# Gate and up products of two experts in one product of 512 moving columns

## The chip, the cores and the metric

The kernel runs on one NeuronCore of a Trainium2 chip. The metric is the time of one execution on the device in microseconds (us), lower being better. The kernel before takes 586.83 us, the median of three runs (585.6 to 587.18). Engines are named as in the profile: PE (TensorE: matrix products, PEld being its weight loads), DVE (VectorE), ACT (ScalarE), POOL (GpSimd) and SP (SyncE, which issues the DMAs).

## The reference

One layer of a perceiver: 256 tokens `x` of width 512 and a context of 25088 rows of width 512. Three blocks, each with a layer norm ahead of it and added to `x`: attention with a sigmoid over the context, causal self-attention with 16 heads, and a feed-forward block of 8 experts. The change touches the last:

```python
logits = jnp.einsum('th,eh->te', xf, gate_w)
onehot = one_hot(argmax(logits, -1), 8)
g = jnp.einsum('th,ehd->etd', xf, wg)        # gate, 8 experts of [512, 128]
u = jnp.einsum('th,ehd->etd', xf, wu)        # up
inter = jnp.square(jax.nn.relu(g)) * u
inter = inter * onehot.T[:, :, None]
out = jnp.einsum('etd,edh->th', inter, wd)   # down, [128, 512] each
```

All eight experts are computed for all tokens; the one-hot factor leaves one of them per token.

## The kernel before

**Split products.** Most large products are made in an fp32r form in which an operand is split into a high part and a low part (`split`, lines 62 to 65: ACT makes the high part, L64, DVE the rest, L65). A product is then three matmuls (`mm3`, lines L68 to L70): high by high, high by low, low by high. Each matmul has a weight load of its own, of 128x128.

**The main loop** goes over the context in 49 chunks of 512 rows. A chunk is loaded twice, transposed and plain (1 MB each), split, projected to keys, scored against the queries, and its sigmoid weights multiply the plain rows into two accumulators `acc`, one per tile of 128 tokens. From the third chunk on, `prepare` does one piece of side work a chunk: it loads 512 columns of a weight matrix that is needed later, splits it, and writes the two halves to a DRAM tensor (`spill`), in pieces of 256 KB on SP's queue. The list `todo` says at which column each half goes: `to` for the high half and `to + apart` for the low half.

**The tail** works on two tiles of 128 tokens, `tt` = 0 and 1. Its order on every engine is the order of the calls at the end of the body, held by `in_order`. The split expert weights come back from DRAM in eight loads of 1 MB (`load_gu`), into one tile `gu[e]` for each `e`. Before, the 2048 columns of `gu[e]` are the high half and the low half of expert `e`; in each half, four blocks of 256 columns follow each other, one for each 128 rows of the contraction, and a block holds 128 gate columns and 128 up columns.

**The experts** go in pairs (0 and 1, 2 and 3, ...). For each pair and token tile:
- `GU(tt, e, 0)` and `GU(tt, e, 1)`: the gate and up products. The normed tokens (`yhl`, high and low) are the weights of the array, the expert weights move through it. Both calls write one PSUM bank of 512 columns, 256 for each expert. For the last pair of the second tile the calls carry `alone`, and each has a bank of its own.
- `GE`: ACT takes the relu, DVE multiplies relu, gate, up and the one-hot factor.
- `IT`: PE transposes the result, ACT and DVE split it into `ft`.
- `DN`: the down product, 6 matmuls of 512 columns for a pair, added up over the experts in `fo`.

The calls are interleaved, so that other PE work stands between a pair's steps; the first gate/up calls lie between transposes and value products of the second tile's attention. The activation of `GE` reads both halves of the bank:

```python
nc.scalar.activation(r[:, ks], p4[:, ks, 0, :], AF.Relu)
```

`ks` covers both experts, except in the last pair. The order of the tail around a pair:

```python
GU(1, 2, 1)
DN(1, 0)
GE(1, 2)
GU(1, 4, 0)
IT(1, 2)
```

Of the kernel before, what the change touches and what calls it, by code (L numbers as in the profile page):

```python
# [22 lines left out]
D = 512  # L23
KD = D // P
# [4 lines left out]
E = 8  # L29
# [19 lines left out]
def body(ctx, tc, a, out, nch=NCH):  # L49
# [17 lines left out]
    def mm3(ps, ahi, alo, bhi, blo, first, last):  # L67
        mm(ps, lhsT=ahi, rhs=bhi, start=first, stop=False)  # L68
        mm(ps, lhsT=ahi, rhs=blo, start=False, stop=False)  # L69
        mm(ps, lhsT=alo, rhs=bhi, start=False, stop=last)  # L70

    def pair(name, shape, tag=None, bufs=1):
        return [sb.tile(shape, F32R, tag=f"{tag or name}{i}", name=f"{name}_{i}", bufs=bufs) for i in range(2)]

    def bank(name):
        return psum.tile([P, D], F32, tag="b", name=name, bufs=6)
# [4 lines left out]
    def toks(t):  # L81
        return slice(t * P, (t + 1) * P)
# [22 lines left out]
    spill = {n: dram.tile([P, 2 * w], F32, name=f"sp_{n}") for n, w in (("wo", KD * D), ("gu", E * 2 * D), ("dn", E * D))}  # L105

    todo = [("wv", at, None, at) for at in range(0, KD * D, D)]
    todo += [("gu", at, 2 * D, at // (2 * D) * 4 * D + at % (2 * D)) for at in range(0, E * 2 * D, D)]
    todo += [("dn", at, D, 2 * at) for at in range(0, E * D, D)]
    todo += [("wo", at, KD * D, at) for at in range(0, KD * D, D)]  # L110

# [194 lines left out]
    for i in range(2):  # L306
        nc.gpsimd.memset(kbd[i], 0.0)
    sums = sm.tile([P, 2, NH], F32, name="sums")


    gu, dn = [None] * E, [None] * E
# [203 lines left out]
    gps, inter = {}, {}  # L515

    def GU(tt, e, i, alone=False):
        if i == 0 or alone:
            gps[tt, e, i] = bank(f"gu{tt}_{e}_{i}").rearrange("p (e w) -> p e w", e=2)
        gps[tt, e, 1] = gps[tt, e, i]  # L520
        w = gu[e + i]
        for j in range(KD):
            s = slice(2 * j * P, 2 * (j + 1) * P)
            mm3(gps[tt, e, i][:, i, :], yhl[0][:, j, toks(tt)], yhl[1][:, j, toks(tt)], w[:, 0, s], w[:, 1, s],
                j == 0, j == KD - 1)

    def GE(tt, e, ks=slice(0, 2)):
# [96 lines left out]
    yhl = pair("y", [P, KD, T], "oh")  # L624
# [25 lines left out]
    PT(1, 5)  # L650
    PT(1, 6)
    GU(0, 0, 0)
    PV(1, 5)
    PT(1, 7)
    R1(1)
    GU(0, 0, 1)
    PV(1, 6)
    PV(1, 7)
    R2(1)
    GU(0, 2, 0)  # L660
    AT(1)
    LG(0)
# [108 lines left out]
```

## Time and profile before

| | |
|---|---|
| median of three runs | 586.83 us (585.6, 586.83, 587.18) |
| profiled execution | 586.28 us, its span 584.5 us |
| PE / PEld / DVE / ACT / POOL busy | 570.6 / 481.7 / 459.7 / 395.1 / 21.1 us |
| gate/up matmuls, 256 columns | 192, from 537.4 to 577.5 us |
| down matmuls, 512 columns | 48, from 552.3 to 580.4 us |
| loads of the split gate/up weights | 8, issued 464.9 to 493.4 us, 4.7 to 7.9 us to landing |
| spill writes of gate/up halves | 32, issued 80.6 to 226.7 us, 2.1 to 7.9 us to landing |

The span runs from the first to the last instruction of the core, and times in the profile count from its start. "L68" is a line of the kernel; `mm3` records all its matmuls under its own three lines, so groups are told apart by the tiles that they write (`gu`, `fo`, `acc`). [...] The lines of the profile stand in the prediction.

### The profile page before, as it was taken

Reading aid. Unit: us, or ns where it says so; the run is one execution under the profiler, and the core shown is the slowest. Engines: PE = TensorE matmul, PEld = TensorE weight load, DVE = VectorE, ACT = ScalarE, POOL = GpSimd, SP = SyncE. Lnnn points to the kernel's source line nnn. Section 1 sums busy time; section 2 is a strip of 40 time slices with the busy share of each in tenths; the row PEclk is TensorE's granted clock in tenths of the full one; section 3 lists DMA queues with packets and bytes.
Section 4 is the critical chain, followed back from the end, with each engine's and each line's share of the span. In section 5 each row is a group of like instructions: output and inputs, shape, how many; then the busy total and the mean of one; then the engine's idle time right before and its main releaser. Section 6 shows DMA issues by size and latency. Waiting matters only on the chain.

```text
span 584.5 us, 8061 instructions
## 1 busy us (share of the span) xinstructions
PE 570.6 (98%) x3036; PEld 481.7 (82%) x3036; DVE 459.7 (79%) x528; ACT 395.1 (68%) x512; POOL 21.1 (4%) x28
## 2 busy tenths in 40 slices
PE   4999999999999999999999999999999999999997
PEld 3888888888888888888888888888888887876996
DVE  6898888888888888888888888787878765667543
ACT  5877777777777777777777776767676752574211
POOL 5200000000000000000000000000000041000000
PEclk9999999999999999999999999999999999999999
DMA  8897887879888888788988887565657477700000
GB/s 288 334 368 283 278 295 281 321 278 317 287 324 276 325 271 325 266 337 298 332 282 319 274 337 245 208 225 206 234 198 243 149 295 262 316 1 1 1 1 36
DMA packets 33526, 144.94 MB, mean 248 GB/s; under 512 B 4240, under 2 KB 4432, under 8 KB 19792
## 3 DMA queue, kind: packets, MB, share of 16 engines
q1 hardware_dynamic: 33488, 144.44, 69.3%
q8 instruction: 23, 0.38, 0.2%
q14 instruction: 15, 0.12, 0.1%
HBM read 129.22 MB, written 15.20 MB: 247 GB/s over the span
## 4 chain that ended last, share of the span: by engine, by line
PE 95%; DVE 3%; DMA 1%; issue 0%; POOL 0%; ACT 0%; SPq 0%; POOLq 0%
PE acc L68 15%; PE acc L69 15%; PE acc L70 15%; PE kp_ps L70 8%; PE kp_ps L69 8%; PE kp_ps L68 8%; PE sc L70 4%; PE sc L69 4%; PE sc L68 4%; PE s L428 2%; PE gu L68 1%; PE gu L69 1%; PE gu L70 1%; PE pt L445 1%; DMA wq_r<-in_wq 1%; PE pv L456 1%
## 5 line engine op out<-in xcount | busy, mean ns | idle before, releaser
L68 PE MATMUL acc<-N,z 128*128 128x512 f32 x392 | 153.9, 393 | 0.0
L69 PE MATMUL acc<-N,z 128*128 128x512 f32 x392 | 153.7, 392 | 0.0
L65 DVE TENSOR_TENSOR N<-rN,N 128x2048 fp32r<-128x2048 f32 (+1 forms) x53 | 111.6, 2110 | 52.3 <-ACT N L64 52.2
L70 PE MATMUL acc<-N,z 128*128 128x512 f32 x392 | 152.5, 389 | 0.0
L65 DVE TENSOR_TENSOR T<-rT,T 128x2048 fp32r<-128x2048 f32 (+1 forms) x49 | 110.3, 2252 | 15.3 <-ACT T L64 15.3
L187 ACT ACTIVATE z<-sc 128x512 f32<-128x512 f32 x98 | 58.7, 599 | 66.5 <-PE sc L70 66.2
L64 ACT CAST N<-rN 128x2048 fp32r<-128x2048 f32 (+1 forms) x55 | 94.4, 1725 | 6.1
L64 ACT CAST T<-rT 128x2048 fp32r<-128x2048 f32 (+1 forms) x55 | 94.3, 1721 | 0.9 <-DMA rT<-in_ctxT 0.7
L70 PEld LDWEIGHTS acc<-N,z 128*128 128x128 f32 x392 | 73.6, 188 | 16.0
L68 PEld LDWEIGHTS acc<-N,z 128*128 128x128 f32 x392 | 74.0, 189 | 12.3
L69 PEld LDWEIGHTS acc<-N,z 128*128 128x128 f32 x392 | 74.0, 189 | 11.7
L68 PE MATMUL kp_ps<-T,wk 128*128 128x512 f32 x196 | 76.9, 392 | 0.0
L70 PE MATMUL kp_ps<-T,wk 128*128 128x512 f32 x196 | 76.7, 392 | 0.0
L69 PE MATMUL kp_ps<-T,wk 128*128 128x512 f32 x192 | 74.7, 389 | 0.0
L189 DVE TENSOR_TENSOR zacc<-zacc,z 128x512 f32<-128x512 f32 x98 | 67.2, 686 | 3.7 <-ACT z L187 1.7
L65 DVE TENSOR_TENSOR z<-z,z 128x512 fp32r<-128x512 f32 x98 | 67.3, 686 | 0.0
L64 ACT CAST z<-z 128x512 fp32r<-128x512 f32 x98 | 61.0, 623 | 3.1
L178 ACT ACTIVATE kp<-kp_ps,bk 128x512 fp32r<-128x512 f32 x49 | 33.9, 691 | 39.9 <-PE kp_ps L70 39.9
L70 PE MATMUL sc<-qp,kp 128*128 128x256 f32 x196 | 55.8, 285 | 0.1
L69 PE MATMUL sc<-qp,kp 128*128 128x256 f32 x196 | 55.4, 283 | 0.0
L68 PE MATMUL sc<-qp,kp 128*128 128x256 f32 x196 | 54.9, 280 | 0.0
L68 PEld LDWEIGHTS kp_ps<-T,wk 128*128 128x128 f32 x196 | 37.1, 189 | 7.8
(177 smaller groups left out, 658.5 us busy)
## 6 DMA issues: line engine op xcount, KB each, us to landing
rN<-in_ctxN SPq DMA_DIRECT2D x49, 1024.0 KB, 5.7
rT<-in_ctxT SPq DMA_DIRECT2D x47, 1024.0 KB, 5.5
sp_gu<-w_gu SPq DMA_DIRECT2D x32, 256.0 KB, 4.3
gu<-sp_gu SPq DMA_DIRECT2D x8, 1024.0 KB, 6.0
r_gu<-in_gu SPq DMA_DIRECT2D x16, 256.0 KB, 5.7
sp_dn<-w_dn SPq DMA_DIRECT2D x16, 256.0 KB, 4.3
dn<-sp_dn SPq DMA_DIRECT2D x16, 256.0 KB, 6.0
r_dn<-in_dn SPq DMA_DIRECT2D x8, 256.0 KB, 6.1
```

The lines of the kernel that those rows point to most:

```text
L64: copy(hi, src)
L65: eng.tensor_tensor(lo, src, f(hi), ALU.subtract)
L68: mm(ps, lhsT=ahi, rhs=bhi, start=first, stop=False)
L69: mm(ps, lhsT=ahi, rhs=blo, start=False, stop=False)
L70: mm(ps, lhsT=alo, rhs=bhi, start=False, stop=last)
L178: nc.scalar.activation(kp[c][0], ps, AF.Identity, bias=bk)
L187: nc.scalar.activation(z, ps, AF.Sigmoid, scale=1.0 / math.sqrt(128.0))
L189: tt2(zacc, zacc, z, ALU.add)
L428: mm(p3[:, h - h0:h - h0 + 2, :], lhsT=qs[:, tt, h // 2, g, :], rhs=kbd[g // 2][:, g % 2, h:h + 2, :nk], start=tt == 1, stop=tt == 0 and h ...
L445: nc.tensor.transpose(ps[:, toks(i * (tt + 1) + kt)], pr[tt, u][:, i, toks(kt)], ident)
L456: mm(pv[tt][r, g, :], lhsT=vs[kt][:, g * P + r.start:g * P + r.stop], rhs=pt[tt, u][:, toks(i * (tt + 1) + kt)], start=kt == 0, stop=kt == tt)
```

## The change

The DRAM layout of the split gate/up weights is regrouped by pairs: for a pair `e`, `e + 1`, the tile `gu[e]` now holds the high halves of both experts, and `gu[e + 1]` the low halves of both. Sizes, loads and their order stay.

A call of `GU` that is not `alone` now takes both experts at once: the moving operand is `gu[e][:, 0:2, s]`, two runs of 256 columns that lie 1024 columns apart, and the output is the whole bank of 512 columns. The first call of a pair does the contraction blocks 0 and 1, the second the blocks 2 and 3. Each such call has 6 matmuls of 512 columns in place of 12 of 256. The two calls with `alone` keep 12 matmuls of 256 columns, taken from the new places.

```diff
-    todo += [("gu", at, 2 * D, at // (2 * D) * 4 * D + at % (2 * D)) for at in range(0, E * 2 * D, D)]
+    todo += [("gu", at, 4 * D, at // (4 * D) * 8 * D + at % (4 * D)) for at in range(0, E * 2 * D, D)]
...
         gps[tt, e, 1] = gps[tt, e, i]
-        w = gu[e + i]
-        for j in range(KD):
+
+        for j in (range(KD) if alone else (2 * i, 2 * i + 1)):
             s = slice(2 * j * P, 2 * (j + 1) * P)
-            mm3(gps[tt, e, i][:, i, :], yhl[0][:, j, toks(tt)], yhl[1][:, j, toks(tt)], w[:, 0, s], w[:, 1, s],
+            k = slice(i, i + 1) if alone else slice(0, 2)
+            mm3(gps[tt, e, i][:, k, :], yhl[0][:, j, toks(tt)], yhl[1][:, j, toks(tt)], gu[e][:, k, s], gu[e + 1][:, k, s],
                 j == 0, j == KD - 1)
```

## The prediction

> **What bounds the kernel now.** I read the page first: the busy line, the clock row and the chain that ended last. Lines left out are marked.
>
> ```profile
> PE 570.6 (98%) x3036; PEld 481.7 (82%) x3036; DVE 459.7 (79%) x528; ACT 395.1 (68%) x512; POOL 21.1 (4%) x28
> ...
> PEclk9999999999999999999999999999999999999999
> ...
> PE 95%; DVE 3%; DMA 1%; issue 0%; POOL 0%; ACT 0%; SPq 0%; POOLq 0%
> ```
>
> TensorE (PE) is busy for 98% of the span, its clock is full in every slice, and the chain is 95% PE. An average can hide a stage with another limit, so I cut the span at the stage that the change touches. In the table of stretches the columns are length, then busy time (and count) of PE, PEld, DVE, ACT and POOL, then clock, DMA share and GB/s.
>
> ```profile
> 460.00:537.00 77.00, 75.30 (x473) 58.39 (x472) 51.72 (x93) 41.92 (x109) 9.51 (x8) 1.00 0.47 177
> 537.00:578.00 41.00, 41.00 (x315) 38.05 (x314) 20.17 (x56) 9.10 (x25) 0.55 (x1) 1.00 0.02 7
> 578.00:584.50 6.50, 2.83 (x14) 1.90 (x12) 1.92 (x5) 0.68 (x3) 0.00 (x0) 1.00 0.10 40
> ```
>
> The changed products all lie in the second row. There PE has no gap at all (41.00 of 41.00 us), DVE and ACT are half idle or more, and the DMA engines are nearly silent. So what PE saves there comes off the end, unless a wait appears where none is now.
>
> What is a matmul worth? The group rows give about 283 to 298 ns for a gate/up matmul of 256 columns and about 392 to 405 ns for one of 512. Those are latencies that overlap, and taken as costs they would promise 84 x (2 x 288 - 397) = 15 us. The true price is the distance between starts, so I read PE's timeline and the stretches of whole calls. First a down call (6 matmuls of 512 columns), then the gate/up call behind it (12 of 256), then the transpose that follows:
>
> ```profile
> 568.71:570.09 1.38, 1.38 (x8) 1.13 (x7) 0.73 (x3) 0.38 (x1) 0.00 (x0) 1.00 0.00 0
> 570.09:571.53 1.44, 1.44 (x13) 1.43 (x12) 0.30 (x2) 0.00 (x0) 0.00 (x0) 1.00 0.00 0
> ```
>
> ```profile
> 570.09 0.28 PE L68 MATMUL gu<-gu,y 128*128 128x256 f32 x1
> 570.21 0.28 PE L69 MATMUL gu<-gu,y 128*128 128x256 f32 x1
> ...
> 571.53 0.38 PE L541 MATMUL it<-ident,f 128*128 128x128 f32 x2
> ```
>
> Each matmul lasts 0.28 us, but the next starts 0.12 us later. The undisturbed gate/up calls take 1.44, 1.44 and 1.43 us (starts 562.56, 570.09, 574.58): 1.437/12 = 119.7 ns per matmul. The down calls at 561.17, 565.66, 568.71 and 573.19 take 1.39, 1.39, 1.38 and 1.39 us: 1.3875/6 = 231.3 ns. Both shapes move the same columns in a call: 12 x 256 = 6 x 512. The weight loads fill all of the 256-column call (1.43 us) and 1.13 of 1.38 us of the 512-column one; in both they lie under matmuls.
>
> **What the Trainium skill says.** "TensorE: Matmul & The Clock Gate", section "Back-to-back issue gap", prices an isolated warm gap at N/2.4 + 2.5 ns: about 109 ns for 256 columns and 216 for 512. So one 512 saves only one fixed issue cost (2.5 ns) against two 256. The trace agrees in kind and is dearer: 119.7 and 231.3, a saving of 2 x 119.7 - 231.3 = 8.1 ns. The measured pair is used. The same page, section "Step-by-step: what each phase is for", says that weight loads are pulled ahead of running matmuls; the trace shows this too. "SBUF — State Buffer" says that strided reads pay when successive accesses leave a 16-byte line, and that non-contiguous PSUM patterns slow matmuls. Here each run of the moving operand is 256 fp32 (1 KB), with one jump between two runs, and the output is a whole contiguous bank, so neither should bite. No row of before shows a split-weight product with this exact operand.
>
> **The change part by part.**
> 1. The calls. Of the 16 calls of the gate/up function, 14 change from 12 matmuls of 256 columns to 6 of 512: 168 matmuls and their weight loads become 84. The last two, marked alone, keep 12 of 256 (24 matmuls). Removed: 168 x 119.7 ns = 20.11 us. Added: 84 x 231.3 ns = 19.43 us. Sum: -0.68 us, or 49 ns a call. The first matmul behind a short PE operation has a bubble (0.20 instead of 0.12 us to the next after the transpose at 564.00; 0.31 instead of 0.23 us in the down call at 579.20): 0.08 us for either width, with as many such places as before, so nothing.
> 2. The moving operand in two runs, 4 KB apart in the partition. Its cost is unknown for these products. The nearest rows are attention scores for the first token tile (two runs of 128 columns, plain fp32) against the second (one run of 512):
>
> ```profile
> 505.14 1.03 PE L428 MATMUL s<-kbd,qs 128*128 128x256 f32 x4
> 506.00 0.38 PE L426 MATMUL s<-mask,identb 128*128 128x512 bf16 x1
> ...
> 521.17 1.02 PE L428 MATMUL s<-kbd,qs 128*128 128x512 f32 x2
> 522.03 0.27 PE L431 MATMUL s<-mask,identb 128*128 128x256 bf16 x1
> ```
>
> Four passes of 256 take 0.86 us, two of 512 take 0.86 us: a jump costs nothing visible. These passes run at about half the rate, which could hide a jump; the bf16 mask product (the same 128 columns four times, so four runs) starts at 504.93 and gives way at 505.14: 512 columns in 0.21 us. I take 0. Bounds: -15.6 ns per matmul (231.3 becomes the page's 215.7), which adds 1.3 us of gain as an estimate from that page; above, 8.1 ns, where two runs cost as much as two matmuls and the gain is gone. More than that no row suggests.
> 3. Order of accumulation. The first call of a pair now takes half the contraction for both experts, and the second call the rest. The activation behind a pair waits for both calls before and after, so it is not later. The first call needs two weight tiles instead of one; the eight loads are issued between 464.9 and 493.4 us and land within 7.9 us, the first use is at 537.4: 36 us of cover.
> 4. Addresses of the spilled halves in DRAM. 32 writes of 256 KB and 8 loads of 1 MB stay, with the same run lengths, order and queue; nothing passes anything else on SP's queue. They issue at 80.6 to 226.7 us and land in 7.9 us at most. A staging buffer is taken again two chunks later, and a chunk lasts about 9.8 us ((460-20)/45), so a slow write must lose some 10 us to be seen. Cost 0.
> 5. Cover that shrinks. A call is 49 ns shorter, so what hides under it has 49 ns less. No new wait is added, but on PE's in-order queue a late input would hold all that follows. The tightest place is the down product at 565.66, whose transposed input DVE finishes at 564.87 + 0.42 = 565.29: 0.37 us of slack becomes 0.32. At 568.71 and 573.19 it is 0.42. The transposes of the second tile's attention at 542.22 need a copy that DVE ends at 541.62: 0.60 becomes 0.50 behind two shorter calls. All hold, so cost 0; if one failed it would give back at most a call's 0.05 us.
>
> Sum: -0.68 us. Against the profiled execution: span 584.5 to 583.8, its time 586.28 (1.78 us around the span, which nothing touches) to 585.6. The shown runs are 585.6, 586.83 and 587.18; the profiled execution is 0.55 below their median. From the median: 586.83 - 0.7 = 586.1.
>
> **The rivals.**
> A. Larger gain. 512-column products run at 215.7 ns. Gain 84 x (239.4 - 215.7) = 2.0 us, 584.8. Against: the 48 down matmuls, with the same fp32r type and alternating weights, keep 231 ns, as do the main loop's products.
> B. Gain swallowed. A chain of transpose, ACT, DVE and down product becomes the bound, and PE waits for the 49 ns of each call: 586.8. For it: these chains are the only waits near. Against: the smallest slack that is left, 0.32 us, is over six times the step.
> C. Slower. The jump stalls the moving stream in all 84 products. Place: PE between 537 and 572 us. It is slower than before from 8.1 ns each, and by over 0.3% (1.76 us) from (1.76 + 0.68)/84 = 29 ns: 260 ns per matmul, 588.6. Against: the rows of point 2.
> That the change doesn't do what it says is excluded for counts and widths, which the code fixes; only its worth is open.
>
> **How the numbers follow.** About 0.3% is what a measurement of this kernel can tell from no change. Chances: the small gain 0.74, B 0.12, A 0.06, C 0.05, and 0.03 that medians of few runs (they spread over 1.6 us before) make the small gain look over 0.3%. The first two fall within 0.3%: 0.86; A and the spread make faster 0.09; C is slower 0.05. The small gain with the spread of the runs gives 585.3 to 586.9; the range reaches 585.0 towards A and 587.3 for B with a high run.
>
> **What would show it.** Right: 84 gate/up matmuls of 512 columns 230 to 233 ns apart, calls of 1.39 us, the stage 0.7 us shorter, PE still without gaps. Wrong: starts over 240 ns apart (C), 216 to 220 (A), PE idle before a down product or a transpose (B), or a main loop that moves by more than 0.3 us (point 4).

## The result and the profile after

The changed kernel takes 585.03 us (median of 22 runs, 584.1 to 585.89), the kernel before 586.05 us (also the median of 22 runs). The ratio is 0.9982, with a 95% interval of 0.9975 to 0.9988: faster by 0.12 to 0.25%. The profiled execution has a span of 582.7 us, against 584.5.

The page of the changed kernel, its busy line, clock and chain:

```profile
PE 568.9 (98%) x2952; PEld 476.3 (82%) x2952; DVE 459.9 (79%) x528; ACT 395.1 (68%) x512; POOL 21.2 (4%) x28
...
PEclk9999999999999999999999999999999999999999
...
PE 94%; DVE 3%; DMA 1%; issue 0%; POOL 0%; ACT 0%; SPq 0%; POOLq 0%
```

84 matmuls and 84 weight loads are gone (3036 to 2952), and PE still carries the chain. For the stage itself, the fairest stretch runs from the start of the first gate/up matmul to the start of the last down matmul. In the table of stretches of the kernel before:

```profile
537.43:580.43 43.00, 43.00 (x322) 39.52 (x321) 20.97 (x59) 9.73 (x27) 0.55 (x1) 1.00 0.02 7
```

and of the changed kernel:

```profile
536.41:578.63 42.22, 42.22 (x238) 34.80 (x237) 20.97 (x59) 9.73 (x27) 0.55 (x1) 1.00 0.02 7
```

The stage became 0.78 us shorter. PE has no gap in either, so no wait took the place of the removed work; DVE and ACT do the same work to the hundredth. The rest of the 1.8 us between the two spans was there before the first gate/up product started: 537.43 against 536.41, so 1.02 us. That part is not the change. At the first key product (`kp_ps`) it is 0.26 us (10.33 against 10.07), at the first accumulator product of the main loop already 1.08 us (20.91 against 19.83), and behind the loop 1.02 us (482.35 against 481.33). Most of it arises between 10 and 15 us. PE's timeline in the kernel before:

```profile
12.61 0.63 PE L70 MATMUL kp_ps<-T,wk 128*128 128x512 f32 x1
13.04 0.41 PE L68 MATMUL qp_ps<-xa,wq 128*128 128x256 f32 x1
13.25 0.41 PE L69 MATMUL qp_ps<-xa,wq 128*128 128x256 f32 x1
```

and in the changed kernel:

```profile
12.35 0.42 PE L70 MATMUL kp_ps<-T,wk 128*128 128x512 f32 x1
12.61 0.28 PE L68 MATMUL qp_ps<-xa,wq 128*128 128x256 f32 x1
12.73 0.28 PE L69 MATMUL qp_ps<-xa,wq 128*128 128x256 f32 x1
```

The same products start 0.43 and 0.21 us apart in the first, and 0.26 and 0.12 us apart in the second. In the execution before, PE ran at the slow clock until 14.5 us; in that of the changed kernel, until 12.4 us. The Trainium skill tells of this in "TensorE: Matmul & The Clock Gate", section "What's actually happening": the clock starts throttled and is released by a free-running activity window, so the moment varies between runs. The traces agree. Their record of the granted clock begins with the step to full speed, at 14.49 and 12.39 us; the table of stretches reads 1.00 ahead of it only because nothing is recorded there. In the four traces of the first four experiments below, which have the same start, the step comes between 13.46 and 14.79 us. Two of those kernels have the wide products, and they reach the experts at 537.30 and 537.41 us, as late as the kernel before: the early start does not come with the change.

The stage in calls. The stretches of the changed kernel are a down call, a gate/up call behind it, and a gate/up call behind a transpose:

```profile
559.70:561.08 1.38, 1.38 (x8) 1.13 (x7) 0.73 (x3) 0.00 (x0) 0.00 (x0) 1.00 0.00 0
561.08:562.45 1.37, 1.37 (x8) 1.08 (x7) 0.00 (x0) 0.00 (x0) 0.00 (x0) 1.00 0.00 0
562.58:564.05 1.47, 1.47 (x9) 1.21 (x8) 0.73 (x2) 0.66 (x2) 0.00 (x0) 1.00 0.00 0
```

The same three calls of the kernel before:

```profile
561.17:562.56 1.39, 1.39 (x9) 1.13 (x7) 0.70 (x3) 0.00 (x0) 0.00 (x0) 1.00 0.00 0
562.56:564.00 1.44, 1.44 (x14) 1.44 (x13) 0.00 (x0) 0.00 (x0) 0.00 (x0) 1.00 0.00 0
564.13:565.66 1.53, 1.53 (x16) 1.53 (x14) 0.76 (x2) 0.66 (x2) 0.00 (x0) 1.00 0.00 0
```

Behind the transpose the call saves 0.05 us (1.527 to 1.474 by starts that the trace keeps to the ns; the lines round), near the predicted 0.049. Behind another call of 512 columns it saves 0.07, and takes 1.37 us where the prediction had 1.39. Two down calls became shorter too, those at 551.01 and 571.40 us: 1.37 and 1.36 us instead of 1.39.

```profile
571.40:572.76 1.36, 1.36 (x7) 1.13 (x6) 0.71 (x3) 0.39 (x1) 0.00 (x0) 1.00 0.00 0
```

The four other down calls of six matmuls (554.43, 559.70, 564.05 and 567.05 us) also stand directly behind 512-column products now, and keep 1.38 to 1.39 us.

### The profile page after: what moved, and what is told of

It is laid out like the page before. It is cut to its first block, busy times and chain, and to the rows that moved or that the text cites. A ratio compares the mean times of both kernels' runs of the same rounds, so it can differ in the third digit from the quotient of the medians.

```text
span 582.7 us, 7892 instructions
## 1 busy us (share of the span) xinstructions
PE 568.9 (98%) x2952; PEld 476.3 (82%) x2952; DVE 459.9 (79%) x528; ACT 395.1 (68%) x512; POOL 21.2 (4%) x28
## 4 chain that ended last, share of the span: by engine, by line
PE 94%; DVE 3%; DMA 1%; issue 0%; POOL 0%; ACT 0%; SPq 0%; POOLq 0%
PE acc L68 15%; PE acc L69 15%; PE acc L70 15%; PE kp_ps L68 8%; PE kp_ps L69 8%; PE kp_ps L70 8%; PE sc L70 4%; PE sc L69 4%; PE sc L68 4%; PE s L429 2%; PE gu L68 1%; PE gu L70 1%; PE gu L69 1%; PE pt L446 1%; DMA wq_r<-in_wq 1%; PE pv L457 1%
```

## The experiments

My theory is the prediction's: two matmuls of 256 columns cost more than one of 512, by an amount per pair. The rivals are the regrouped DRAM addresses, a price for the jump in the moving operand, and chance at the start of the run.

**The grouping alone.** All gate/up products stay at 256 columns, taken from the new places.

```diff
-        for j in (range(KD) if alone else (2 * i, 2 * i + 1)):
+        for j in range(KD):
...
-            k = slice(i, i + 1) if alone else slice(0, 2)
+            k = slice(i, i + 1)
```

> The new grouping of the spilled halves alone, all gate/up products still of 256 columns. Theory (the width of the products makes the gain): no difference from before, about 586.0 us, ratio 0.9995 to 1.0005, gate/up calls of 1.44 us. Rival (the DRAM addresses or the load grouping make part of it): a gain of 0.3 to 1.0 us, ratio 0.998 to 0.9995, with unchanged calls.

Measured: 586.31 us against 586.27 for the kernel before, ratio 0.9999, interval 0.9991 to 1.0007. The stage and an undisturbed call:

```profile
537.02:580.02 43.00, 43.00 (x322) 39.53 (x321) 20.97 (x59) 9.72 (x27) 0.55 (x1) 1.00 0.02 7
562.15:563.59 1.44, 1.44 (x14) 1.44 (x13) 0.00 (x0) 0.00 (x0) 0.00 (x0) 1.00 0.00 0
```

43.00 us and 1.44 us, as before. The interval would allow up to 0.5 us of gain, but the stage shows none. So the gain comes with joining two products into one: with the width, and with the halved number of matmuls and weight loads that goes with it.

**No jump.** The host lays the 256 columns of both experts side by side, block by block; the rest is the changed kernel.

```diff
-    r["gu"] = w.transpose(2, 0, 1, 3).reshape(P, -1)
+    r["gu"] = w.reshape(E // 2, 2, KD, P, 2 * P).transpose(3, 0, 2, 1, 4).reshape(P, -1)
...
+            s = slice((4 * j + 2 * k.start) * P, (4 * j + 2 * k.stop) * P)
...
+                yhl[1][:, j, toks(tt)], hi[:, s], lo[:, s], j == 0, j == KD - 1)
```

> The changed kernel with the columns of a pair put side by side on the host, so that the moving operand of 512 columns is one run without a jump. Theory (the jump is free): the same as the changed kernel, about 585.0 us, calls of 1.37 to 1.39 us where no bubble stands ahead. Rival (the jump costs a few ns in each of the 84 products): calls shorter than in the changed kernel, by 0.05 us a call if it costs 8 ns, and 0.7 us less in all.

Measured: 585.07 us, ratio 0.9982 (0.9973 to 0.9991). The stage and the call that stands behind a down call:

```profile
537.30:579.53 42.23, 42.23 (x239) 34.81 (x237) 20.98 (x59) 9.74 (x27) 0.55 (x1) 1.00 0.02 7
561.97:563.34 1.37, 1.37 (x7) 1.08 (x6) 0.00 (x0) 0.00 (x0) 0.00 (x0) 1.00 0.00 0
```

42.23 against 42.22 us: over 84 products the jump costs nothing that the trace resolves.

**The same work five times.** To read the price from a larger sum, each pair that the change widens is computed five times, once in 256-column products on the new grouping and once in 512-column ones. Each pass starts a new accumulation. The first edit is against the kernel with the grouping alone, the second against the changed kernel.

```diff
-        for j in range(KD):
+        for j in [*range(KD)] * (1 if alone else 5):
```

```diff
-        for j in (range(KD) if alone else (2 * i, 2 * i + 1)):
+        for j in (range(KD) if alone else [2 * i, 2 * i + 1] + [*range(KD)] * (4 * i)):
```

> The new grouping with 256-column products, each product of the seven pairs that the change widens done five times (each pass starts afresh, so the values stay): 672 matmuls more. At 119.7 ns each this is 80.4 us more, about 666.5 us.

> The changed kernel with the same four extra passes over each of the seven pairs, in 512-column products: 336 matmuls more. Theory of the prediction (231.3 ns each): 77.7 us more, about 662.9 us, 3.4 us below the 256-column form of the same length. Rival (an unbroken stream of wide products runs at 227 to 228 ns, as a second wide call behind another one does): 76.4 us more, about 661.4 us, 5 us below.

Measured: 666.56 us with 256 columns and 661.9 us with 512, 4.7 us apart. The stage of the 256-column kernel, and one of its calls of 60 matmuls:

```profile
613.86:621.05 7.19, 7.19 (x61) 7.19 (x60) 0.00 (x0) 0.00 (x0) 0.00 (x0) 1.00 0.01 2
536.89:660.54 123.65, 123.65 (x994) 120.16 (x993) 21.07 (x59) 9.73 (x27) 0.55 (x1) 1.00 0.01 3
```

and of the 512-column kernel, with a call of 54 matmuls:

```profile
605.54:617.79 12.25, 12.25 (x55) 10.09 (x54) 0.00 (x0) 0.00 (x0) 0.00 (x0) 1.00 0.00 0
537.41:655.74 118.33, 118.33 (x574) 97.86 (x573) 20.98 (x59) 9.73 (x27) 0.55 (x1) 1.00 0.01 3
```

The stages are 5.32 us apart; the prediction's prices give 3.4 us. The extra passes alone: the gate/up calls of PE's timeline add up to 104.78 us in the 256-column kernel and to 24.14 us in the kernel with the grouping alone, so 80.64/672 = 120.0 ns for 256 columns. For 512 columns it is 99.61 against 23.43 us in the changed kernel, 76.18/336 = 226.7 ns. A pair saves 2 x 120.0 - 226.7 = 13.3 ns in a long stream, where the prediction had 8.1. The 256-column price holds there too; the 512-column price is 4.6 ns lower in the stream. The rival of the last expectation, 76.4 us more, is what came.

**A start with the clock kept up.** Products of zeros that nobody reads are put ahead of the first transposes, in the kernel before and in the changed one.

```diff
+    dummy = bank("dummy")[:, :T]
+    for _ in range(6):
+        mm(dummy, lhsT=zacc[:, 0, :P], rhs=zacc[:, 1, :], start=True, stop=True)
     split(*wk, wk_r, nc.gpsimd)
```

> The kernel before with six products of zeros ahead of its first transposes (fp32, 256 columns, into a bank that nobody reads), while PE has nothing else to do. Theory (the profile of before started its first products at the slow clock until 14.3 us, that of the changed kernel only until 12.4 us, and this start is chance): the first key products start 0.23 us apart instead of 0.43, the time falls by 1 to 1.8 us to 584.4 to 585.2, and the spread of the runs, 1.8 us before, falls below 1 us. Rival (the spread comes from elsewhere): the same time and spread as before.

> The changed kernel with the same six products. Theory: with the chance of the start taken out, it lies below the 256-column kernel with the same start by the 0.78 us that the stage of the experts shows, about 583.6 to 584.4 us. Rival (the change is worth the 1.05 us of the medians, so 0.27 us more lies elsewhere): 1.05 us below it.

Measured: 585.43 us for the first (19 runs, 584.7 to 586.47, ratio 0.9987, 0.9981 to 0.9994) and 584.27 us for the second (5 runs, ratio 0.9962, 0.9948 to 0.9976). The expectation failed at its root: in both traces most of the first key products still started 0.43 us apart. The six products were over at 6.45 and 6.91 us, the transposes leave PE idle for most of the time to 10 us, and the slow clock came back. Here the record of the clock covers it (of the 256-column kernel):

```profile
5.90:9.20 3.30, 1.20 (x7) 0.56 (x5) 2.32 (x5) 1.77 (x4) 2.08 (x3) 1.00 1.00 299
9.30:12.60 3.30, 2.71 (x9) 2.32 (x10) 3.03 (x5) 2.02 (x5) 0.63 (x2) 0.50 1.04 340
```

PE was busy for 1.20 of 3.30 us, and for the next 3.30 us the granted clock is 0.50. The first kernel gained 0.69 us over the kernel before in the same runs, below the expected 1 to 1.8, and its spread stayed at 1.8 us. The second lies 1.16 us below the first by the medians and 1.08 +- 0.32 us by the means (two standard errors): nearer the rival's 1.05 than the 0.78 of the theory, but both lie within the error. The stages are still 43.02 and 42.22 us.

So the second try has eight such products ahead and two more between the two groups of transposes; `busy(n)` makes `n` of them:

```diff
...
+    busy(8)
     split(*wk, wk_r, nc.gpsimd)
...
-    xps = [transposed(bank(f"xa_ps{tt}"), xn[tt]) for tt in range(2)]
+    xps = []
+    for tt in range(2):
+        xps.append(transposed(bank(f"xa_ps{tt}"), xn[tt]))
+        busy(2 - 2 * tt)
```

> The kernel before with eight products of zeros (fp32, 256 columns, read by nobody) ahead of its first transposes and two more behind the first four of them, since six alone were over 1.5 us before the first transpose and the clock fell again. Theory (the start at the slow clock makes the spread of the runs): the first key products start 0.23 us apart, the time falls by 1.3 to 2 us to about 584.4, the runs lie within 1 us. Rival (the spread comes from elsewhere, as the first try would allow): no less spread.

> The changed kernel with the same ten products. Theory (the change is worth what the experts' stage shows, 0.78 us): 0.6 to 0.95 us below the 256-column kernel with the same start, about 583.6 us. Rival (0.27 us more lies outside the stage): 1.05 us or more below it.

Measured: 584.99 us for the 256-column kernel (21 runs, 584.65 to 585.66) and 584.49 us for the changed one (6 runs, 583.88 to 584.73). Now the first key products last 0.39 to 0.50 us instead of 0.63 to 0.78: the fast clock holds. The starts are 0.23 us apart only where no wait lies between, for now PE waits for its operands, as in these stretches of the changed kernel:

```profile
8.00:10.00 2.00, 1.86 (x11) 1.27 (x9) 0.85 (x2) 1.19 (x4) 1.36 (x1) 1.00 1.04 335
10.00:12.00 2.00, 1.54 (x6) 0.90 (x6) 2.00 (x4) 2.00 (x5) 0.35 (x1) 1.00 1.00 379
```

Between 10 and 12 us PE is busy for 1.54 of 2.00 us: ACT and DVE, which split the context, are busy for all of it and set the pace; PE's two waits of 0.23 us there are for DVE. So only part of the slow start can be won: 1.1 us against 1.3 to 2 expected (0.88 +- 0.22 us by the means of the spans). The standard deviation falls from 0.45 us (26 runs of the kernel before) to 0.29 us, that of the spans from 0.47 to 0.29, so the clock at the start makes part of the spread, not all. The stages are 43.00 and 42.22 us once more. The difference of the means is 585.05 - 584.41 = 0.64 us, of the medians 0.50; with standard deviations of 0.29 and 0.30 us and 21 and 6 runs, the mean's difference is uncertain by about 0.28 us (two standard errors). That holds 0.78 us and leaves out 1.05. The changed kernel was expected at about 583.6 us and came out 0.9 us above that. The two tries together, weighted by their errors, give 0.82 +- 0.21 us: 0.78 fits well, and 1.05 lies just outside. The changed kernel with this start has a ratio of 0.9968 to the kernel before (0.9956 to 0.998).

## Why the prediction was right or wrong

**The forecast of "no difference" was wrong, and the step that failed is in "How the numbers follow"**: "about 0.3% is what a measurement of this kernel can tell from no change". I gave 0.86 to no difference on that ground, and 0.09 to faster. The bound had been taken from the spread of three runs, 1.6 us, as if a median over many runs were as uncertain as that. With 22 runs on each side the interval is only 0.13% wide, 0.7 to 1.5 us, and it excludes equality. The stage alone, 0.78 us or 0.13%, is twice the interval's half width.

**The time** of 586.1 us missed by 1.07 us. It was counted from the median of three runs, 586.83 us, where 22 runs gave 586.05: 0.78 us of the miss is this base. That 585.03 us still lies within the range, at its very edge of 585.0, is luck.

**What bounds the kernel** was read rightly. The stage has no PE gap before or after, and what PE saved came off the end: 0.78 us of the stage.

**Point 1, the sum,** came out nearly as forecast: by the starts in the trace the gate/up calls went from 24.14 to 23.43 us, -0.70 us against -0.68. The mechanism is shown: the grouping alone gave nothing, the joined products gave the stage's 0.78 us. On average over these 84 products the price was right as well: with as many bubbles as before it was (20.11 - 0.70)/84 = 231.1 ns. What the prediction missed is that 231.3 is not the price of a 512-column product as such, but of the first ones behind other work. The down calls that it was read from all stand directly behind 256-column products. Twelve 512-column products of the kernel before, the `wo_ps` group, show both prices; here are its first five distances between starts and the next five:

```profile
546.48:547.64 1.16, 1.16 (x7) 0.95 (x6) 1.05 (x4) 0.00 (x0) 0.00 (x0) 1.00 0.00 0
547.64:548.77 1.13, 1.13 (x6) 0.94 (x5) 0.00 (x0) 0.00 (x0) 0.00 (x0) 1.00 0.00 0
```

That is 232 and 227 ns for one. In the main loop between 60 and 300 us the first five distances behind other shapes average 232.2 ns, those from the sixth on 226.7, so the reason given against rival A, that the main loop's products keep 231 ns, was a misreading. In the changed kernel most gate/up calls begin behind a short operation such as a transpose. There the dear distances (224 to 236 ns, 231 to 232 on average, besides the bubble) last for the first seven to ten products, so they fill the call of six and reach into the down call behind it. This is why four down calls kept 1.38 to 1.39 us, and why only calls deeper in a stream take 1.36 or 1.37. At the prices of a long stream the change would have been worth 84 x 13.3 ns = 1.12 us, an estimate from the run that does the work five times.

**A term put at nothing** is the down calls: they do the same work as before, but now stand behind 512-column products, two of them late in such a stream. Together they went from 9.82 to 9.74 us (-0.08), and these two made most of it. With the -0.70 of the gate/up calls this is the stage's 0.78 us.

**Point 2, the jump,** was taken at 0 and measured at 0 (42.23 against 42.22 us). **Rival C**, a stall of 29 ns or more per matmul, is refuted by the same run.

**Point 3,** the order of accumulation, made no wait: in the changed kernel's stage PE is busy for 42.22 of 42.22 us. **Point 4,** the addresses, was rightly nothing: from the first accumulator product to the first product behind it, the main loop took 461.44 us before and 461.50 after, and only its place moved. **Point 5,** the shrinking cover, held: the down product at 564.05 us has its input from DVE at 563.32 + 0.42 = 563.74, a slack of 0.31 us where I had said 0.32. **Rival B** did not come.

**Rival A,** a 512-column price of 215.7 ns and 2.0 us of gain, was too cheap: a long stream in this kernel runs at 226.7 ns. The skill's gap of N/2.4 + 2.5 ns ("Back-to-back issue gap"), which the page gives for an isolated matmul, has too small a fixed cost for this stream. If the price is a fixed share and a share per column, the two measured prices give (226.7 - 120.0)/256 = 0.417 ns per column, which agrees with the page's 2.4 columns per ns, and 120.0 - 256 x 0.417 = 13.3 ns per matmul besides. The pair saves just one such share.

**The rest of the median's difference,** 1.02 us against 0.78, is not explained by the change. The runs show two places where it can come from. One is the start: the slow clock lasted 2.1 us longer in the one profiled execution than in the other, and the main loop began 1.08 us later. With the clock kept up the difference was 0.64 +- 0.28 us. The other is time outside the span, ahead of the first instruction or behind the last. The spans of the kernel before in the first comparison are not on record, but in its 71 later runs this time is 2.01 us on average, and 1.78 us in the 22 runs of the changed kernel. This 0.23 us is not a matter of the width: the kernels with 256-column products of the experiments have 1.77 to 1.86 us. The spans of these 71 and 22 runs differ by 0.97 +- 0.25 us, and the interval of the first comparison, 0.7 to 1.5 us, holds 0.78 as well.

**Open:** why the first matmuls of 512 columns behind shorter ones are about 5 ns dearer each. Weight loads lie under the matmuls in both cases, and no run here separates a cause. That the fixed 13.3 ns belong to the weight loads was not tested either. With the width the order of the contraction blocks between the two experts changed too; it was not tried alone. Why the kernel before spends more time outside its span is not known.

## What to carry to other kernels

Price a matmul by the distance between starts, and sample it in the surroundings that the changed code will have: the same shape cost 232 ns behind other work and 227 in a stream. Halving the number of these fp32r matmuls at equal columns was worth 13 ns for each that goes in a long stream and 8 ns (0.70 us/84) in this kernel's short calls, in a stage where PE has no gaps. And before calling a small change unmeasurable, count the runs: a median over 22 of them saw 0.18%.

## What was not expected

- The fixed cost of a split-weight matmul with a weight load of its own is 13.3 ns, an estimate from 120.0 and 226.7 ns, five times the 2.5 that the skill gives for an isolated one.
- The first 512-column matmuls behind other work are slower by about 5 ns each (232.2 against 226.7 ns on average in the main loop), five of them behind products of 256 columns, the first seven to ten behind short operations.
- A moving operand in two runs 4 KB apart streams as fast as one run.
- The clock at the start came up at 14.49 us in one execution and at 12.39 us in another, and the main loop began 1.08 us apart. The granted clock reads 1.00 ahead of these moments, where the traces have no record of it.
- A difference of 0.23 us between the two kernels' times lies outside the spans, where no profile shows it.
- Six products of zeros up to 6.5 us did not keep the clock up until 10 us; ten, with two of them in the gap between the transposes, did. The kernel before then fell to 584.99 us.
